# A two-layer graph network on one Trainium2 core: V's weight blocks fetched at other points of the queue, and the first iterations re-ordered

## The chip, the core and the metric

The kernel runs on one core of a Trainium2 chip. A core has TensorE (PE, matrix products; a weight load, PEld, goes with each), VectorE (DVE), ScalarE (ACT), GpSimd (POOL) and SyncE (SP), which here only issues transfers. The metric is the device time of one execution in microseconds (us): 2586.28 us, the median of three runs (2578.19 to 2588.11). The profiled execution has a span of 2589.9 us.

## The reference

Two layers on x (128 batches of 128 tokens and 512 features, float32), each with the batch's own 128x128 mask adj.

```python
# layer 0: attention with 8 heads of 64, then Wo and ReLU
q = (x @ Wq + bq); k = (x @ Wk + bk); v = (x @ Wv + bv)       # split into 8 heads
logits = einsum('bqhd,bkhd->bhqk', q, k) / sqrt(64)
attn = softmax(where(adj > 0, logits, -1e9), axis=-1)
o = einsum('bhqk,bkhd->bqhd', attn, v).reshape(b, n, 512)
x = layernorm(x + relu(o @ Wo + bo))
# layer 1: graph attention with one head
Wh = x @ W
e = leaky(Wh @ a[:512] [:, :, None] + Wh @ a[512:] [:, None, :])   # leaky: slope 0.2
attention = softmax(where(adj > 0, e, -9e15), axis=1)
x = layernorm(x + leaky(attention @ Wh))
```

## The kernel before

Iteration t of the main loop works at once on several batches: the logits and softmax of batch t, attention times V of batch t-1, the product with Wo of the pair that begins at t-3 (odd t), the product with W of the pair that begins at t-6 (even t), the second layer's softmax of batch t-7 and its end. Beside these it makes Q, K and V for the next group of four batches. All instructions of an engine run in the order in which the program writes them.

Every large product is a Strassen product: 7 block products instead of 8. A group's chain works in three PSUM banks, y, w and x, whose roles rotate from chain to chain:

```python
def strassen(bank, multiply, read, add):
    p, t = {}, {}
    def p1():
        p["y"] = bank("y"); multiply(p["y"], 0, True); t[0] = read("t0", p["y"], 0)
    def p5():
        p["w"] = bank("w"); multiply(p["w"], 4, True)
    def p6():
        multiply(p["y"], 5, False); t[2] = read("t2", p["y"], 1)
    def p2():
        p["x"] = bank("x"); multiply(p["x"], 1, True); add(0, 0, p["x"], t[0])
    def p7():
        multiply(p["y"], 6, False); t[3] = read("t3", p["y"], 1); add(1, 1, p["w"], t[3])
    def p4():
        multiply(p["y"], 3, False); add(1, 0, p["y"], None)
    def p3():
        multiply(p["w"], 2, False); add(0, 1, p["w"], t[2])
    return [p1, p5, p6, p2, p7, p4, p3]
```

For a group, one such product is 8 matmuls of 128x128 by 128x256 in the trace. `read` is a ScalarE copy of a bank, `add` a VectorE addition (a ScalarE copy for p4). Wq and Wk with their sums stay on chip; Wv's seven blocks lie in device memory (`wv`) and are fetched for each group into three buffers (`wv_n`):

```python
ring, todo = {}, [0, 4, 5, 1, 6, 3, 2]

def fetch():
    if todo:
        n = todo.pop(0)
        ring[n] = work.tile([P, 2, HALF], F32, name="wv_n", bufs=3)
        nc.sync.dma_start(ring[n], wv[n])

def fetched(n):                 # the weight of V's product n
    fetch()
    return ring.pop(n)

chains = [
    group_product(g, 3 * g, lambda n: wq[:, PLACE[n]], features_first(Q), True, b_cols[:, 0, :]),
    group_product(g, 3 * g + 1, lambda n: wk[:, PLACE[n]], features_first(K), True),
    group_product(g, 3 * g + 2, fetched, tokens_first(V), False),
]
# K's first step also fetches two blocks (cut: with_fetch)
order = [chains[0][n] for n in ((0, 3, 1, 2, 4) if g == 0 else range(5))]
for n in range(2):
    order += [chains[n + 1][0], chains[n][6], chains[n][5]]
    order += chains[n + 1][1:5]
return order + chains[2][5:]
```

The 21 steps of a group are spread over four iterations by `group()`, five in each of three and the rest in the fourth (t a multiple of 4). `pair()` does the same for the seven steps of the products with Wo or W, and `group()` also does up to two "chores": the sums of the weight blocks of Wk, Wv, Wo and W on VectorE, the writes of `wv`, the parts of bo in bf16, the products of W with a.

```python
for t in range(-3, B + 9):
    ...                                       # cut: new steps, load of the mask
    last, sm = sm, Softmax(t) if on(t) else none      # logits of batch t
    while later:
        later.pop(0)()                        # store and 8 spread loads (xz) of the pair's x1
    sm.maxima()
    group()
    ...                                       # cut: second layer
    pair()
    sm.exp(0, 1, 2, 3)
    edge.exp()
    pair()
    sm.exp(4, 5)
    last.transpose()                          # paT of batch t-1
    group()
    sm.reciprocals(0)
    sm.exp(6)
    fin.store()                               # store of the output
    pair()
    sm.exp(7)
    ...
    sm.divide(0, 1, 2, 3)
    group()
    sm.divide(4, 5)
    pair()
    sm.divide(6, 7)
    ...
    copy_o = attend(last) if last is not none else none.copy    # p_oT
    if t % 2 == 0:
        copy_o()
    group()
    sm.spread()                               # pa to device memory and back, as paz
    ...                                       # cut: transposes and loads of x for later groups
    pair(2)
    ...
    group(21 if t % GROUP == 0 else 1)
    fin = Finish(edge) if edge is not none else none
```

x is wanted with features on the partitions. It is loaded in pieces of 512 bytes ("spread", one piece for each block of 32 tokens and quarter of the features) and turned by VectorE in blocks of 32x32. The first four batches, ahead of the loop:

```python
xz = load_pair(0, "pa")                       # batches 0 and 1, spread, SyncE queue
load_blocks(Wq, columns(wq), nc.scalar)
...                                           # b_rows: bq and bv, ScalarE queue
xz2 = load_pair(1, "paz")
load_blocks(Wk, columns(wk), nc.sync)
scale(0); transpose_pair(0, xz)
scale(1); transpose_pair(1, xz2)
sum_x(0)                                      # left sums of x on GpSimd
...                                           # cut: scales and sums of Wq on VectorE
turn_biases()                                 # b_cols: transpose of b_rows on TensorE, two VectorE copies
```

Of the kernel before, what the change touches and what calls it, by code (L numbers as in the profile page):

```python
# [15 lines left out]

H = 8
GROUP = 4
CHORES = 2
EPS = 1e-5  # L20
ALPHA = 0.2
BIG = -1e30
# [3 lines left out]
def kernel(  # L26
# [88 lines left out]
        nc.vector.tensor_scalar_mul(b_cols[:, 0, :], p_b[:, :NC], QSCALE)  # L115
        nc.vector.tensor_copy(b_cols[:, 1, :], p_b[:, NC : 2 * NC])

    def load_blocks(w, columns, queue, spread_rows=True):

        for o, t in enumerate(columns):  # L120
            if spread_rows:
                rows = w.rearrange("(q k c i) (o f) -> o q i k c f", q=4, k=2, c=2, o=2)
                for q in range(4):
                    queue.dma_start(t[32 * q : 32 * q + 32, :, :, :HALF], rows[o, q])
            else:
                rows = w.rearrange("(k c p) (o f) -> o k p c f", k=2, c=2, o=2)
                for k in range(2):
                    queue.dma_start(t[:, k, :, :HALF], rows[o, k])
# [4 lines left out]
    def right_blocks(t):  # L133

        return [
            lambda: nc.vector.tensor_sub(t[2], t[2], t[0]),
            lambda: nc.vector.tensor_sub(t[5], t[3], t[2]),
            lambda: nc.vector.tensor_sub(t[4], t[5], t[0]),
            lambda: nc.vector.tensor_sub(t[6], t[1], t[5]),
        ]  # L140

    def places(w):
        return [w[:, n] for n in range(7)]

    def columns(w):
        return w[:, 0:2], w[:, 2:4]
# [43 lines left out]
    def load_w1():  # L190

        load_blocks(W1, columns(w1), nc.sync)
        a_b = work.tile([P, 2, D], F32, name="a_b", tag="x1T")
        nc.sync.dma_start(
            a_b.rearrange("p s f -> p (s f)"),
            a1.rearrange("f o -> (f o)").partition_broadcast(P),
        )
        sums = small.tile([P, 2, 2, 2, 2], F32, name="wa", bufs=1)

        def dots(k, o, c):  # L200
            def run():
                for s in range(2):
                    scr = work.tile([P, HALF], F32, name="wa_scr", tag="y")
                    nc.vector.scalar_tensor_tensor(
                        scr,
                        w1[:, 2 * o + k, c, :HALF],
                        1.0,
                        a_b[:, s, o * HALF : (o + 1) * HALF],
                        op0=ALU.mult,
                        op1=ALU.mult,  # L210
                        accum_out=sums[:, s, k, o, c : c + 1],
                    )

            return run

        def last_column(k, o):
            def run():
                for c in range(2):
                    nc.vector.tensor_add(
                        w1[:, 2 * o + k, c, HALF:],  # L220
                        sums[:, o, k, 0, c : c + 1],
                        sums[:, o, k, 1, c : c + 1],
                    )

            return run

        every = [(k, o) for k in range(2) for o in range(2)]
        ops = [dots(k, o, c) for k, o in every for c in range(2)]
        return ops + [last_column(k, o) for k, o in every] + right_blocks(places(w1))
# [33 lines left out]
    def sum_x(g):  # L263
        sums = big.tile([P, 3, 2, 2 * P], F32, name="xS")
        XS[g] = left_blocks(XT[g], sums)

    def load_pair(pair, tag):

        z = work.tile([P, 2, 4, P], F32, name="xz2", tag=tag)
        block = x[2 * pair : 2 * pair + 2].rearrange("b (a i) (q e) -> q i (b a) e", i=32, q=4)  # L270
        for q in range(4):
            nc.sync.dma_start(
                z[32 * q : 32 * q + 32].rearrange("p b a e -> p (b a) e"), block[q]
            )
        return z

    def left_blocks(xT, sums):

# [97 lines left out]
    def products(g):  # L376

        for h in range(2):
            Q[g, h] = big.tile([P, NC, HALF], F32, name="qT", bufs=4)
            K[g, h] = big.tile([P, NC, HALF], F32, name="kT", bufs=3)  # L380
            V[g, h] = big.tile([P, 2, D], F32, name="v", bufs=3)

        def features_first(dst):
            return lambda h, o: dst[g, h][:, 2 * o : 2 * o + 2, :]

        def tokens_first(dst):
            return lambda h, o: dst[g, h][:, :, o * HALF : (o + 1) * HALF]
# [6 lines that stand above are left out]
                ring[n] = work.tile([P, 2, HALF], F32, name="wv_n", bufs=3)  # L394
                nc.sync.dma_start(ring[n], wv[n])

        def fetched(n):
            fetch()
            return ring.pop(n)

        chains = [
            group_product(g, 3 * g, lambda n: wq[:, PLACE[n]], features_first(Q), True, b_cols[:, 0, :]),
            group_product(g, 3 * g + 1, lambda n: wk[:, PLACE[n]], features_first(K), True),
            group_product(g, 3 * g + 2, fetched, tokens_first(V), False),
        ]
        fetch_first = chains[1][0]

        def with_fetch():
            fetch_first()
            fetch()  # L410
            fetch()

        chains[1][0] = with_fetch

        order = [chains[0][n] for n in ((0, 3, 1, 2, 4) if g == 0 else range(5))]
        for n in range(2):
            order += [chains[n + 1][0], chains[n][6], chains[n][5]]
            order += chains[n + 1][1:5]
        return order + chains[2][5:]

    def pair_product(xs, w, add, bias=None):
# [294 lines left out]
    group_steps = []  # L716
    later = []
    chores = []
    sm = fin = none

    x_turns = [(), (7, 8), (8,), (8,)]


    xz = load_pair(0, "pa")
    load_blocks(Wq, columns(wq), nc.scalar)
    nc.scalar.dma_start(b_rows[:NC, :], bq.rearrange("(c p) -> c p", p=P))
    nc.scalar.dma_start(b_rows[NC:, :], bv.rearrange("(c p) -> c p", p=P))
    xz2 = load_pair(1, "paz")
    load_blocks(Wk, columns(wk), nc.sync)
    XT[0] = big.tile([P, NC, GROUP * P], F32, name="xT")  # L730

    def transpose_pair(pair, z):
        nc.vector.transpose(
            XT[0][:, :, 2 * pair * P : 2 * (pair + 1) * P].rearrange(
                "p c (b i) -> p b c i", i=32
            ),
            z.rearrange("p b a (c i) -> p (b a) c i", i=32),
        )

    def scale(n):  # L740
        nc.vector.tensor_scalar_mul(wq[:, n], wq[:, n], QSCALE)

    wq_sums = right_blocks(places(wq))
    scale(0)
    transpose_pair(0, xz)
    scale(1)
    transpose_pair(1, xz2)
    sum_x(0)
    scale(2)
    wq_sums[0]()  # L750
    scale(3)
    for op in wq_sums[1:]:
        op()
    turn_biases()
    load_x(4)
    load_x(5)
    chores += right_blocks(places(wk)) + load_wv()
    for t in range(-3, B + 9):
        pair_steps = []
# [7 lines left out]
        def group(n=1):  # L767
            for _ in range(min(n, len(group_steps))):
                group_steps.pop(0)()
            for _ in range(min(CHORES, len(chores))):  # L770
                chores.pop(0)()

        def pair(n=1):
# [2 lines left out]

        if on(t + 1):
            load_mask(t + 1)
        if t == -2:
            load_blocks(Wo, columns(wo), nc.sync, spread_rows=False)  # L780
            more_chores = right_blocks(places(wo)) + load_bias()
        if t == -1:
            chores += more_chores
            more_chores = load_w1()
        if t == 0:
            chores += more_chores

        last, sm = sm, Softmax(t) if on(t) else none
        while later:
            later.pop(0)()  # L790
        sm.maxima()
        group()
        edge = EdgeSoftmax(t - 7) if on(t - 7) else none
        fin.residual()
        if on(t - 2):
            load_residual(t - 2)
        edge.maxima()
        fin.stats()
        if t % GROUP == 0 and on(t + GROUP):
            sum_x(t // GROUP + 1)  # L800
        pair()
        sm.exp(0, 1, 2, 3)
        edge.exp()
        pair()
        sm.exp(4, 5)
        last.transpose()
        group()
        sm.reciprocals(0)
        sm.exp(6)
        fin.store()  # L810
        pair()
        sm.exp(7)
        edge.divide()
        pair()
        sm.reciprocals(1)
        sm.divide(0, 1, 2, 3)
        group()
        sm.divide(4, 5)
        pair()
        sm.divide(6, 7)  # L820
        if on(t + 1):
            mask_float(t + 1)
        copy_o = attend(last) if last is not none else none.copy
        if t % 2 == 0:
            copy_o()
        group()
        sm.spread()
        for b in x_turns[t % GROUP]:
            if on(t + b):
                transpose_x(t + b)  # L830
        for b in x_turns[(t + 1) % GROUP]:
            if on(t + 1 + b):
                load_x(t + 1 + b)
        if on(t + 1):
            mask(t + 1)
        pair(2)
        if t % 2 == 1:
            copy_o()
        if t % 2 == 0:
            for b in (t - 4, t - 3):  # L840
# [44 lines left out]
```

## Time and profile before

| engine or stretch | busy or length |
|---|---|
| TensorE products | 2457.6 us of 2589.9 |
| TensorE products from 134.4 to 2454.3 us | 2266.05 us of 2319.90, granted clock 0.99 |
| before the first product | 13.7 us |
| iteration 0 (48.9 to 69.3 us) | TensorE 15.27, VectorE 16.10, ScalarE 7.95 us of 20.40 |
| iterations 1, 2, 3 | 11.20, 14.20, 17.40 us long |
| iteration 4 (112.1 to 134.4 us) | TensorE 15.11 us of 22.30 |
| after the last group's V (2454.3 us to the end) | TensorE 90.90 us of 135.60 |
| DMA engines from 0 to 20 us | 98% busy, 194 GB/s |

How such lines are read: a row of waits names the engine, tile and line that waited, what released it, the total in us, how often and the longest. A row of a timeline gives start and length, then engine, line, operation, what it writes and reads, and in brackets the idle time just before it and what ended it. SPq is the issue of transfers on SyncE, which takes its entries strictly in order.

### The profile page before, as it was taken

How to read it: one execution, taken by the hardware profiler on the slowest of the kernel's cores; microseconds unless marked ns; L12 is line 12 of the kernel's file. 1: busy time of each engine (PE TensorE's matmuls, PEld its weight loads, DVE VectorE, ACT ScalarE, POOL GpSimd, SP SyncE). 2: the span in 40 equal slices, each digit the busy share in tenths (PEclk: the TensorE clock that was granted, in tenths of full speed). 3: DMA queues.
4: the chain of work that ended last, by engine and by line, in shares of the span. 5: the costliest groups of instructions: out<-in, count | busy, mean ns of one | idle time of the engine just before them, and what ended most of it. 6: DMA issues, size and time to landing. Idle time of an engine off the chain costs nothing.

```text
span 2589.9 us, 43731 instructions
## 1 busy us (share of the span) xinstructions
PE 2457.6 (95%) x13697; PEld 2007.5 (78%) x13697; DVE 1815.5 (70%) x3754; ACT 1440.9 (56%) x5185; POOL 777.7 (30%) x1161
## 2 busy tenths in 40 slices
PE   6899999999999999999999999999999999999975
PEld 5687888888878888888788778888777888887853
DVE  6566777777777776776776667777677777776675
ACT  2555556556556556556565556556555656555651
POOL 1123233323323323323323333323233323233222
PEclk9999999999999999999999999999999999999987
DMA  7444444544544444444544444444444444544431
GB/s 189 142 133 144 162 146 150 162 139 145 165 136 152 162 138 149 161 143 149 165 143 143 146 136 155 164 138 149 153 136 157 158 139 146 162 144 141 150 126 48
DMA packets 352710, 379.90 MB, mean 147 GB/s; under 512 B 39000, under 2 KB 257120, under 8 KB 352480
## 3 DMA queue, kind: packets, MB, share of 16 engines
q1 hardware_dynamic: 351312, 376.07, 45.1%
q8 instruction: 109, 1.79, 0.3%
q10 hardware_dynamic: 1168, 1.05, 0.2%
q14 instruction: 121, 0.99, 0.1%
HBM read 240.91 MB, written 136.05 MB: 146 GB/s over the span
## 4 chain that ended last, share of the span: by engine, by line
PE 67%; DVE 12%; DMA 8%; issue 4%; SPq 3%; ACT 3%; POOL 1%; DVEq 0%; POOLq 0%; ACTq 0%
PE st_y L354 18%; PE p_y L433 12%; PE st_w L354 10%; PE st_x L354 7%; PE p_w L433 6%; PE p_oT L540 4%; PE lg L477 4%; DMA wv_n<-wv 3%; SPq L239 3%; PE p_h L680 3%; DMA x_dram<-x 3%; DVE st L567 3%; PE p_x L433 2%; DVE x L586 2%; DVE xT L244 2%
## 5 line engine op out<-in xcount | busy, mean ns | idle before, releaser
L572 POOL TENSOR_SCALAR ve<-mv 128x1 f32<-128x1 f32 x256 | 68.8, 269 | 1385.4 <-DVE mv L569 1385.4
L498 ACT ACTIVATE pa<-pa,nmax 128x128 f32<-128x128 f32 x1024 | 399.6, 392 | 44.8 <-DVE nmax L492 38.4
L512 ACT ACTIVATE pa<-pa,rs 128x128 f32<-128x128 f32 x1024 | 339.4, 394 | 42.8 <-DVE rs L508 42.8
L553 ACT ACTIVATE oT<-p_oT,b_cols 128x128 f32<-128x128 f32 x512 | 146.0, 368 | 208.5 <-PE p_w L433 203.6
L486 DVE TENSOR_TENSOR pa<-lg,mf 128x512 f32<-128x512 f32 x256 | 164.5, 684 | 102.4 <-PE lg L477 98.2
L331 ACT COPY st_t<-st_y 128x512 f32<-128x512 f32 x192 | 110.5, 575 | 175.6 <-PE st_y L354 171.7
L477 PEld LDWEIGHTS lg<-kT,qT 64*128 64x128 f32 x2048 | 124.2, 187 | 93.7 <-issue 93.7
L498 ACT ACTIVATION_READ_ACCUMULATOR pa<-pa,nmax 128x1 f32 x1024 | 193.3, 189 | 0.0
L444 ACT COPY pr_t<-p_y 128x256 f32<-128x256 f32 (+1 forms) x384 | 140.1, 365 | 88.9 <-PE p_y L433 82.2
L574 POOL TENSOR_TENSOR rstd<-ve,mhalf 128x1 f32<-128x1 f32 x256 | 176.8, 691 | 21.3
L527 DVE STREAM_TRANSPOSE paT<-paz 128x1024 f32<-128x1024 f32 x128 | 159.4, 1245 | 3.3 <-DMA paz<-pa_dram 3.3
L492 DVE TENSOR_REDUCE nmax<-pa 128x8 f32<-128x1024 f32 x128 | 156.2, 1220 | 4.4
L680 PE MATMUL p_h<-wh,att 128*128 128x512 f32 x256 | 133.9, 605 | 17.5 <-DVE att L671 17.5
L640 DVE TENSOR_TENSOR wh<-p_w,pr_t 128x257 f32<-128x257 f32 x128 | 54.6, 426 | 136.3 <-ACT pr_t L444 69.7
L477 PE MATMUL lg<-kT,qT 64*128 64x128 f32 x2048 | 148.7, 285 | 0.0
L335 ACT ACTIVATE st_t<-st_y,b_cols 128x256 f32<-128x256 f32 x192 | 80.6, 471 | 120.8 <-PE st_y L354 120.7
L540 PEld LDWEIGHTS p_oT<-paT,v 128*64 128x64 f32 x2048 | 111.5, 139 | 45.3 <-issue 42.4
L372 DVE TENSOR_TENSOR v<-st_w,st_t 128x512 f32<-128x512 f32 x64 | 44.3, 692 | 144.1 <-ACT st_t L331 85.3
L433 PE MATMUL p_y<-w,x1S 128*128 128x257 f32 x512 | 134.4, 385 | 10.5 <-ACT pr_t L444 10.5
L540 PE MATMUL p_oT<-paT,v 128*64 128x128 f32 x2048 | 142.8, 282 | 1.5 <-DVE paT L527 1.5
L433 PE MATMUL p_y<-wo,oS 128*128 128x256 f32 x512 | 132.6, 382 | 7.1 <-ACT pr_t L444 7.1
L654 ACT ACTIVATE e<-p_e,wh 128x128 f32<-128x128 f32 x128 | 47.3, 370 | 161.3 <-PE p_e L652 161.3
(147 smaller groups left out, 6058.7 us busy)
## 6 DMA issues: line engine op xcount, KB each, us to landing
pa_dram<-pa SPq DMA_DIRECT2D x128, 512.0 KB, 2.6
paz<-pa_dram SPq DMA_DIRECT2D x512, 128.0 KB, 2.7
wv_n<-wv SPq DMA_DIRECT2D x224, 256.0 KB, 2.9
x<-in_x_dram SPq DMA_DIRECT2D x128, 256.0 KB, 3.0
x_dram<-x SPq DMA_DIRECT2D x128, 256.0 KB, 2.0
xz<-x_dram SPq DMA_DIRECT2D x512, 64.0 KB, 2.0
out_dram<-z SPq DMA_DIRECT2D x128, 256.0 KB, 2.1
xz<-in_x_dram SPq DMA_DIRECT2D x496, 64.0 KB, 2.2
```

The costliest lines, as they stand in the source:

```text
L354: nc.tensor.matmul(p[:, m, :], lhs, rhs, start=start and m == 0 and kc == 0, stop=True, skip_group_check=True,)
L433: nc.tensor.matmul(p[:, :width], xs[n][:, kc, :], w[:, PLACE[n], kc, :], start=start and kc == 0, stop=True, skip_group_check=True,)
L477: nc.tensor.matmul(self.lg[r][:, c, :], q[rows, c, cols], k[rows, c, cols], start=True, stop=True)
L486: nc.vector.tensor_add(by_head[:, r * NC : (r + 1) * NC], self.lg[r].rearrange("p c (b k) -> p c b k", b=4), mf.unsqueeze(1).to_broadcast( ...
L492: nc.vector.tensor_reduce(self.nmax, by_head, AX.XY, ALU.max, negate=True)
L498: nc.scalar.activation(self.pa[:, :, h, :], self.pa[:, :, h, :], AF.Exp, bias=self.nmax[:, h : h + 1], accum_out=self.sums[:, h : h + 1],)
L512: nc.scalar.activation(self.pa[:, :, h, :], self.pa[:, :, h, :], AF.Copy, scale=self.rs[:, h : h + 1])
L527: nc.vector.transpose(self.paT.rearrange("p h (a i) -> p a h i", i=32), self.paz.rearrange("p a (h k) -> p a h k", k=32),)
L540: nc.tensor.matmul(p[r * HD : (r + 1) * HD, c, :], v[:, h * HD : (h + 1) * HD], sm.paT[:, r * NC + c, :], start=True, stop=True,)
L553: nc.scalar.activation(OT[pair][:, c, h * P : (h + 1) * P], p[:, c, :], AF.Identity, bias=b_cols[:, 1, c : c + 1],)
L574: nc.gpsimd.tensor_tensor(rstd, ve, mhalf, ALU.pow)
L680: nc.tensor.matmul(p.rearrange("p (o f) -> p o f", o=2), edge.att, wh, start=True, stop=True)
```

## The change

Three things. Within a group, V's blocks are fetched at the end of named steps instead of at the start of V's own, so that block 1 is fetched with K's fourth product (the last step of the third iteration) and not with V's second (in the fourth); and Q's products 4 and 3 change places. The first four batches of x are loaded in whole rows, their features put in order by a VectorE copy, and turned by TensorE with an identity; half of Wq is loaded from the SyncE queue. The iterations before t = 3, which have no product with Wo or W, get a timetable of their own, and the chores are spread otherwise: Wo's from iteration 0, W's from iteration 2. The aim is that TensorE should not wait for V's blocks, for K's bank or for the first data.

```diff
-        def fetched(n):
-            fetch()
-            return ring.pop(n)
...
-            group_product(g, 3 * g + 2, fetched, tokens_first(V), False),
+            group_product(g, 3 * g + 2, ring.pop, tokens_first(V), False),
...
+        def with_fetch(step, n=1):
+            def run():
+                step()
+                for _ in range(n):
+                    fetch()
+            return run
+        chains[1][0] = with_fetch(chains[1][0], 2)
+        chains[2][0] = with_fetch(chains[2][0])
+        chains[1][5] = with_fetch(chains[1][5])
+        for n in (1, 2, 3):
+            chains[2][n] = with_fetch(chains[2][n])
 
         order = [chains[0][n] for n in ((0, 3, 1, 2, 4) if g == 0 else range(5))]
-        for n in range(2):
-            order += [chains[n + 1][0], chains[n][6], chains[n][5]]
-            order += chains[n + 1][1:5]
+        order += [chains[1][0], *chains[0][5:], *chains[1][1:5]]
+        order += [chains[2][0], chains[1][6], chains[1][5], *chains[2][1:5]]
         return order + chains[2][5:]
...
-    xz = load_pair(0, "pa")
-    load_blocks(Wq, columns(wq), nc.scalar)
+    x_rows = [work.tile([P, 2, D], F32, name="x_rows", tag=tag) for tag in ("pa", "paz")]
+    for b in range(GROUP):
+        nc.sync.dma_start(x_rows[b // 2][:, b % 2, :], x[b])
+    load_blocks(Wq, columns(wq), nc.scalar, only=0)
...
-    xz2 = load_pair(1, "paz")
+    load_blocks(Wq, columns(wq), nc.sync, only=1)
...
+    def order_features(b):
+        rows = x_rows[b // 2][:, b % 2, :]
+        turned = work.tile([P, D], F32, name="x_turned", tag="xz", bufs=3)
+        nc.vector.tensor_copy(
+            turned.rearrange("p (c q i) -> p c q i", q=4, c=4),
+            rows.rearrange("p (q c i) -> p c q i", q=4, c=4),
+        )
+        return turned
+    def transpose_rows(b, turned, copy):
+        p = psum("p_x").rearrange("p (c k) -> p c k", c=NC)
+        for c in range(NC):
+            nc.tensor.transpose(p[:, c, :], turned[:, c * P : (c + 1) * P], ident)
+        copy(XT[0][:, :, b * P : (b + 1) * P], p)
...
+    turned = [order_features(b) for b in range(2)]
+    transpose_rows(0, turned[0], nc.vector.tensor_copy)
+    transpose_rows(1, turned[1], nc.scalar.copy)
+    turned.append(order_features(2))
     scale(0)
-    transpose_pair(0, xz)
+    transpose_rows(2, turned[2], nc.scalar.copy)
+    turned.append(order_features(3))
     scale(1)
-    transpose_pair(1, xz2)
+    transpose_rows(3, turned[3], nc.vector.tensor_copy)
+    turn_biases()
     sum_x(0)
...
-            for _ in range(min(CHORES, len(chores))):
+            for _ in range(min(3 * n if t == -3 else n, len(chores))):
                 chores.pop(0)()
...
-        if t == -2:
+        if t == -1:
             load_blocks(Wo, columns(wo), nc.sync, spread_rows=False)
-            more_chores = right_blocks(places(wo)) + load_bias()
-        if t == -1:
-            chores += more_chores
-            more_chores = load_w1()
-        if t == 0:
-            chores += more_chores
+            late_chores = right_blocks(places(wo)) + load_bias()
+        if t == 1:
+            late_chores = load_w1()
+        if t in (0, 2):
+            chores += late_chores
...
+        if t < 3:
+            sm.maxima()
+            group(2)
+            ...
+            sm.exp(0, 1, 2, 3)
+            last.transpose()
+            group()
+            sm.reciprocals(0)
+            sm.exp(4, 5, 6, 7)
+            sm.reciprocals(1)
+            sm.divide(0, 1, 2)
+            group()
+            copy_o = attend(last) if last is not none else none.copy
+            sm.divide(3, 4)
+            copy_o()
+            sm.divide(5, 6, 7)
+            ...
+        else:
+            ...                      # the timetable of before, unchanged
```

More of the change, by code (lines that the diff above doesn't have):

```diff
@@ L18 @@
 GROUP = 4
-CHORES = 2
 EPS = 1e-5
@@ L116, in turn_biases, with load_blocks @@
         nc.vector.tensor_copy(b_cols[:, 1, :], p_b[:, NC : 2 * NC])
-    def load_blocks(w, columns, queue, spread_rows=True):
+    def load_blocks(w, columns, queue, spread_rows=True, only=None):
         for o, t in enumerate(columns):
+            if only not in (None, o):
+                continue
             if spread_rows:
@@ L202, in run @@
                 for s in range(2):
-                    scr = work.tile([P, HALF], F32, name="wa_scr", tag="y")
+                    scr = work.tile([P, HALF], F32, name="wa_scr", tag="x1S")
                     nc.vector.scalar_tensor_tensor(
@@ L265, in sum_x @@
         XS[g] = left_blocks(XT[g], sums)
[L267 to L275, printed above, removed]
     def left_blocks(xT, sums):
@@ L403, in products @@
             group_product(g, 3 * g + 1, lambda n: wk[:, PLACE[n]], features_first(K), True),
-            group_product(g, 3 * g + 2, fetched, tokens_first(V), False),
+            group_product(g, 3 * g + 2, ring.pop, tokens_first(V), False),
         ]
[L406 to L413, printed above, removed]
+        def with_fetch(step, n=1):
[9 more added lines that the diff above has]
+            chains[2][n] = with_fetch(chains[2][n])
         order = [chains[0][n] for n in ((0, 3, 1, 2, 4) if g == 0 else range(5))]
-        for n in range(2):
-            order += [chains[n + 1][0], chains[n][6], chains[n][5]]
-            order += chains[n + 1][1:5]
+        order += [chains[1][0], *chains[0][5:], *chains[1][1:5]]
+        order += [chains[2][0], chains[1][6], chains[1][5], *chains[2][1:5]]
         return order + chains[2][5:]
@@ L718, with x_turns @@
     chores = []
-    sm = fin = none
-    x_turns = [(), (7, 8), (8,), (8,)]
-    xz = load_pair(0, "pa")
-    load_blocks(Wq, columns(wq), nc.scalar)
+    sm = fin = edge = none
+    def x_turns(t):
+        if t < -1:
+            return () if t == -3 else (4, 5, 6)
+        return [b for b in [(), (t + 7, t + 8), (t + 8,), (t + 8,)][t % GROUP] if on(b)]
+    x_rows = [work.tile([P, 2, D], F32, name="x_rows", tag=tag) for tag in ("pa", "paz")]
+    for b in range(GROUP):
+        nc.sync.dma_start(x_rows[b // 2][:, b % 2, :], x[b])
+    load_blocks(Wq, columns(wq), nc.scalar, only=0)
     nc.scalar.dma_start(b_rows[:NC, :], bq.rearrange("(c p) -> c p", p=P))
     nc.scalar.dma_start(b_rows[NC:, :], bv.rearrange("(c p) -> c p", p=P))
-    xz2 = load_pair(1, "paz")
+    load_blocks(Wq, columns(wq), nc.sync, only=1)
     load_blocks(Wk, columns(wk), nc.sync)
     XT[0] = big.tile([P, NC, GROUP * P], F32, name="xT")
[L732 to L737, printed above, removed]
-        )
+    def order_features(b):
[4 more added lines that the diff above has]
+            rows.rearrange("p (q c i) -> p c q i", q=4, c=4),
+        )
+        return turned
[4 more added lines that the diff above has]
+        copy(XT[0][:, :, b * P : (b + 1) * P], p)
     def scale(n):
@@ L753 @@
         op()
-    turn_biases()
-    load_x(4)
-    load_x(5)
     chores += right_blocks(places(wk)) + load_wv()
@@ L790 @@
             later.pop(0)()
[L791 to L824, printed above, removed]
-            copy_o()
-        group()
-        sm.spread()
-        for b in x_turns[t % GROUP]:
-            if on(t + b):
-                transpose_x(t + b)
@@ L831 @@
-        for b in x_turns[(t + 1) % GROUP]:
-            if on(t + 1 + b):
-                load_x(t + 1 + b)
+        if t < 3:
+            sm.maxima()
+            group(2)
+            if on(t - 2):
+                load_residual(t - 2)
+            if t == 0 and on(GROUP):
+                sum_x(1)
+            sm.exp(0, 1, 2, 3)
[8 more added lines that the diff above has]
+            sm.divide(3, 4)
+            copy_o()
+            sm.divide(5, 6, 7)
+            if on(t + 1):
+                mask_float(t + 1)
+        else:
+            sm.maxima()
+            group()
+            edge = EdgeSoftmax(t - 7) if on(t - 7) else none
+            fin.residual()
+            if on(t - 2):
+                load_residual(t - 2)
+            edge.maxima()
+            fin.stats()
+            if t % GROUP == 0 and on(t + GROUP):
+                sum_x(t // GROUP + 1)
+            pair()
+            sm.exp(0, 1, 2, 3)
+            edge.exp()
+            pair()
+            sm.exp(4, 5)
+            last.transpose()
+            group()
+            sm.reciprocals(0)
+            sm.exp(6)
+            fin.store()
+            pair()
+            sm.exp(7)
+            edge.divide()
+            pair()
+            sm.reciprocals(1)
+            sm.divide(0, 1, 2, 3)
+            group()
+            sm.divide(4, 5)
+            pair()
+            sm.divide(6, 7)
+            if on(t + 1):
+                mask_float(t + 1)
+            copy_o = attend(last) if last is not none else none.copy
+            if t % 2 == 0:
+                copy_o()
+            group()
@@ L834 @@
+        sm.spread()
+        for b in x_turns(t):
+            transpose_x(b)
+        for b in x_turns(t + 1):
+            load_x(b)
         if on(t + 1):
@@ L836 @@
         pair(2)
-        if t % 2 == 1:
+        if t % 2 == 1 and t >= 3:
             copy_o()
```

## The prediction

> **What bounds the kernel now.** I read the page's busy line first, then the table of waits of TensorE alone, then the timelines of TensorE and of the SyncE queue around one typical wait, and last the first 135 us in order of time.
>
> ```profile
> PE 2457.6 (95%) x13697; PEld 2007.5 (78%) x13697; DVE 1815.5 (70%) x3754; ACT 1440.9 (56%) x5185; POOL 777.7 (30%) x1161
> ...
> PE st_x L354 <- DMA wv_n<-wv: 55.3, 31, 6.5
> PE p_y L433 <- ACT pr_t L444: 19.2, 9, 5.0
> PE p_h L680 <- DVE att L671: 17.5, 3, 6.6
> PE p_b L114 <- DMA b_rows<-in_L_gnn_bv_dram: 13.7, 1, 13.7
> PE st_w L354 <- ACT qT L335: 7.6, 30, 1.6
> PE st_y L354 <- ACT st_t L331: 5.8, 3, 2.6
> PE st_y L354 <- issue: 3.8, 2, 2.8
> ```
>
> TensorE is busy 95% of the span and no other engine over 70%, so a microsecond in which TensorE stands still is a microsecond of the span. The waits (total, times, longest) say where it stands. The first row is the great one: `st_x<-wv_n`, the fourth product of V's chain, waits for the fetch of Wv's block 1 in 31 of the 32 groups. The `qT` row is small but comes in 30 groups. `p_y` and `p_h` lie mostly after 2470 us, where no group is left; the change does not touch them. The others lie before 135 us.
>
> Why that fetch is late shows in a steady group (TensorE, then the SyncE queue; columns are start and length in us):
>
> ```profile
> 1278.01 1.03 PE L433 MATMUL p_y<-w,x1S 128*128 128x257 f32 x4
> 1278.88 1.03 PE L433 MATMUL p_x<-w,x1T 128*128 128x257 f32 x4
> 1282.26 1.99 PE L354 MATMUL st_x<-wv_n,xT 128*128 128x256 f32 x8 [2.35 <-DMA wv_n<-wv]
> ```
>
> ```profile
> 1272.34 0.34 SPq L594 DMA_DIRECT2D x_dram<-x  x1
> 1272.72 0.43 SPq L456 DMA_DIRECT2D adj<-in_adj_dram  x1
> 1273.65 1.03 SPq L594 DMA_DIRECT2D x_dram<-x  x1
> 1275.79 3.64 SPq L239 DMA_DIRECT2D xz<-x_dram  x8
> 1279.53 0.38 SPq L395 DMA_DIRECT2D wv_n<-wv  x1
> ```
>
> The block's buffer has long been free (V's first product ended some 16 us before), yet its fetch is issued at 1279.53, behind a store that waits for a normalisation and behind eight issues of 3.64 us that wait for that store to land. The fetch then takes 2.7 us. So this is a place in a queue, not a lack of buffers or of bandwidth.
>
> **What the Trainium skill says.** "Perfetto Trace Analysis", Identifying Performance Opportunities: a gap that repeats on the engine that should be saturated can mean too few buffers. Here the gap repeats, but the trace names another cause, the queue's order. The same page, Identifying the Most-Contended Engine, warns that matmul busy share says little of the distance to the limit; I therefore go by waits and not by the 95%. "TensorE: Matmul & The Clock Gate", Part 1: the array's clock is halved after an idle window of about 3.4 us and needs about as long to return. The trace agrees in kind: of the 31 waits, seven (6.51, 2.92, 3.01, 3.39, 1.91, 3.19 and 3.75 us) are followed by a `st_x` of 3.4 to 3.8 us in place of 1.99, though 1.91 us was once enough and 3.44 us once was not. So a wait can cost more than itself. "DMA: Bandwidth & Descriptors", Issuing engines are not separate DMA queues: issuing from ScalarE and SyncE saves only issue time. So shifting half of Wq from one queue to the other can change which data come first, not how fast they come; in the first 20 us the DMA engines are 98% busy in the trace.
>
> **Part 1: the fetches of V.** The number of fetches stays 7 a group. The order of instructions of the changed kernel shows block 1's fetch on the SyncE queue after the first `x_dram` store and ahead of `adj`, the second store and the eight `xz` issues. By the timeline it would be issued at about 1272.7 instead of 1279.5 and land at 1275.4; the product could begin at 1279.9 (1282.26 - 2.35), so it has 4 us to spare. The wait goes: 55.3 us. With it goes the slow clock after seven of them: (3.60+3.44+3.68+3.78+3.50+3.52+3.53) - 7 x 1.99 = 11.1 us. Sum 66.4 us.
> What takes its place: block 6 now stands in the queue where block 1 stood, and lands where block 1 did. Its product comes after `st_x` (1.73 us at the usual spacing), one pair product (0.86) and `p_oT` (1.02), 3.6 us after `st_x` could start. The median wait of block 1 was about 1.2 us, the longest in the steady part 3.75. So block 6 is in time in all but one or two groups. Blocks 3 and 2 come 0.9 and 4 us later and are wanted 3.5 and 7 us later. I give back 5 us for such cases and for waits of ScalarE or VectorE that the gap used to hide. Net 61 us.
>
> **Part 2: Q's last two products change places.** Before, Q's product 4 (the one that frees bank `y`) ran immediately before K's second product, which takes that bank, and ScalarE's read-out had to fit between. Afterwards product 3 stands between, 1.73 us. The 30 waits go: 7.6 us. Product 4 itself needs only ScalarE's copy of `t3`, and K's first product still lies between. Net 7 us.
>
> **Part 3: the start.** The first product of the first group begins at 13.87 us, slow; the first logits come 35 us later, at 48.92, with 30.4 us of products between.
>
> ```profile
> 13.87 3.75 PE L354 MATMUL st_y<-xT,wq 128*128 128x256 f32 x8
> 17.45 1.91 PE L354 MATMUL st_x<-xT,wq 128*128 128x256 f32 x8
> 19.19 1.89 PE L354 MATMUL st_w<-xS,wq 128*128 128x256 f32 x8
> 23.92 3.40 PE L354 MATMUL st_y<-xS,wq 128*128 128x256 f32 x8 [2.84 <-issue]
> ...
> 57.98 3.38 PE L354 MATMUL st_y<-wv_n,xS 128*128 128x256 f32 x8 [2.53 <-ACT st_t L331]
> 63.97 2.56 PE L354 MATMUL st_y<-wv_n,xT 128*128 128x256 f32 x8 [2.60 <-ACT st_t L331]
> ```
>
> Added are 16 TensorE transposes of 128x128 (273 ns alone for the same operation in `p_e`, about 0.11 us apart back to back; estimate 16 x 0.25 = 4 us with the slow clock), four feature-order copies and four evacuations, 128x512, about 0.65 us each, six of the eight on VectorE: 4 us. Removed are two VectorE transposes of 1.24 us. All of this starts when x comes, and x now comes in whole rows, in front of all but half of Wq, 1.5 MB where 2 MB stood before it. At the 194 GB/s of the first 20 us, 1.5 MB is 7.7 us; with the last copy, transposes and evacuation about 10.5 us. So the first product starts 3 us earlier. b_cols is now computed ahead of the Wq sums (before, ScalarE waited for it until 21.7 us, then loaded its table for 1.28 us, and the fourth product could begin only at 23.9), which I count at 4 us; the gaps before the fifth product and K's second, and the rest of the slow clock, 2 us. The first logits then come near 40 us: 9 us.
> Iteration 0 lasts 20.4 us before (48.92 to 69.31) for 1.1 + 6 x 1.73 = 11.5 us of products; the late ones wait for ScalarE's copies behind exponentials that themselves wait for VectorE, which is doing bias parts and the products with a. Fewer extra jobs there and two steps before the exponentials: I expect 15.5 us, so 5 us. Iteration 2's wait of 1.3 us for `p_oT`: 1 us. Against it, the 16 products with a (551 ns each, 8.8 us of VectorE) and the W sums now fall into iterations 2 to 4, where VectorE has its softmax: I charge 2 us. Net 9 + 5 + 1 - 2 = 13 us.
>
> **Sum.** 61 + 7 + 13 = 81 us. 2586.3 - 81 = 2505 us, a gain of 3.1%.
>
> **The rivals.**
> (a) Another wait takes the gap's place: block 6's fetch, or ScalarE's `st_t` for the fifth product, or VectorE's `paT` for `p_oT`. For: everything near this point is tightly packed, and the copy of `st_t` sits among exponentials. Against: in the group shown `st_t` ended at 1280.1 and is wanted at 1283.5, `paT` ended at 1280.4 and is wanted at 1282.5; and the other three iterations of a group run without any wait. If half of the gap came back, 61 becomes 30 and the time 2536.
> (b) The start gets no better: TensorE's transposes run slow, VectorE takes on 4 us where it was already the one waited for, or DMA, at 98%, decides. The write-out of Wv could also come too late for V's first product. For: the share of DMA. Against: fewer bytes precede the first product. Part 3 would be 0 and the time 2518.
> (c) TensorE, denser, is granted less clock. Against: from 134 to 2454 us it is busy 2266 of 2320 us at a clock of 0.99, and the low clocks lie only after gaps. If it lost 2% of those 2320 us, the gain would fall to 35 us: 2551.
> (d) Better than thought: no give-back and a first logit at 36 us: 2494.
>
> **Range and chances.** The 66 us of part 1 rest on a named wait and a place in a queue that the changed order shows gone; part 3 is the soft term, 0 to 20 us. With (a) half true I get 2536, with (d) and a kinder start about 2485. Range 2484 to 2536. A gain of over 2% means below 2534.6: chance 0.88. Within 2%: 0.10. Slower by over 2%: 0.02.
>
> **What would show it.** Right: the row `st_x <- DMA wv_n` is gone from TensorE's waits and no `wv_n` row over 10 us stands there; its `qT` row is gone; `st_x` products of over 3 us are gone in the steady part; a group takes 75.6 us (76.9, the spacing of groups with a wait near 1.07, less 1.07 and 0.2) where the mean was 77.7; the first logits begin at 38 to 42 us and those of iteration 1 at 54 to 58 us. Wrong: a new row `st_y <- DMA wv_n` of tens of us (a), first logits after 46 us (b), a clock below 0.97 in the steady part (c).

## The result, and the profile after

The changed kernel takes 2515.36 us (median of four runs, 2512.16 to 2516.03). The ratio to the kernel before is 0.9723 (95% interval 0.9693 to 0.9753), a gain of about 72 us. Run again with the last experiments it gave 0.9706 (0.9692 to 0.9720). Foreseen were 2505 us and a gain of 81.

TensorE's share of busy time and the chain that ended last, from the page of the changed kernel, then the waits of TensorE alone (total, times, longest, in us):

```profile
PE 2444.2 (97%) x13713; PEld 2000.3 (80%) x13713; DVE 1817.5 (72%) x3758; ACT 1429.8 (57%) x5187; POOL 781.1 (31%) x1161
...
PE 92%; DVE 3%; DMA 2%; ACT 1%; issue 1%; SPq 1%; POOL 0%; DVEq 0%; POOLq 0%; ACTq 0%
```

```profile
PE p_y L425 <- ACT pr_t L436: 20.3, 11, 5.0
PE p_h L672 <- DVE att L663: 17.6, 3, 6.6
PE p_x L743 <- DVE x_turned L733: 8.0, 4, 5.2
PE p_oT L532 <- DVE paT L519: 3.6, 4, 1.8
PE st_y L345 <- ACT pa L504: 2.6, 1, 2.6
PE st_y L345 <- ACT st_t L322: 2.4, 2, 1.7
PE st_y L345 <- DMA wv_n<-wv: 1.8, 2, 1.6
...
PE st_x L345 <- DMA wv_n<-wv: 0.7, 1, 0.7
```

The great row of before, 55.3 us of `st_x` for block 1, is 0.7 us and one occurrence. The `qT` row is gone. The two rows now on top lie in the last iterations, as before (but for one wait of 0.75 us). In the chain TensorE has 92% where it had 67%.

One steady group of the changed kernel, TensorE and the SyncE queue (start, length):

```profile
1317.08 1.03 PE L425 MATMUL p_x<-w,x1T 128*128 128x257 f32 x4
1317.95 1.89 PE L345 MATMUL st_x<-wv_n,xT 128*128 128x256 f32 x8
1319.67 1.03 PE L425 MATMUL p_y<-w,x1S 128*128 128x257 f32 x4
1320.63 1.09 PE L532 MATMUL p_oT<-paT,v 128*64 128x128 f32 x16
```

```profile
1310.53 0.34 SPq L586 DMA_DIRECT2D x_dram<-x  x1
1310.97 0.38 SPq L386 DMA_DIRECT2D wv_n<-wv  x1
1311.40 0.45 SPq L448 DMA_DIRECT2D adj<-in_adj_dram  x1
1311.90 0.43 SPq L586 DMA_DIRECT2D x_dram<-x  x1
1312.62 3.99 SPq L240 DMA_DIRECT2D xz<-x_dram  x8
1316.71 0.38 SPq L386 DMA_DIRECT2D wv_n<-wv  x1
```

Block 1 (first `wv_n`) is issued at 1310.97, 7 us before `st_x` begins, without a gap. Block 6 (second `wv_n`) stands where block 1 stood, and is issued 5 us ahead of its product. From group to group `st_x` is now 75.63 us apart, the same to 0.02 us for 28 groups; before it was 76.8 to 80.5 from the third group on.

The first logits begin at 43.25 us (before 48.92), those of iterations 1 to 5 at 57.31, 69.80, 83.84, 102.24 and 121.64 (before 69.31, 80.45, 94.66, 112.07, 134.28). So 12.6 us of the gain are in by iteration 5, and the fetch has its part in them.

### The profile page after: what moved, and what is told of

Read it like the earlier page. It is cut to its first block, busy times and chain, and to the rows that moved or that the text cites. A ratio compares the mean times of both kernels' runs of the same rounds, so it can differ in the third digit from the quotient of the medians.

```text
span 2513.0 us, 43768 instructions
## 1 busy us (share of the span) xinstructions
PE 2444.2 (97%) x13713; PEld 2000.3 (80%) x13713; DVE 1817.5 (72%) x3758; ACT 1429.8 (57%) x5187; POOL 781.1 (31%) x1161
## 4 chain that ended last, share of the span: by engine, by line
PE 92%; DVE 3%; DMA 2%; ACT 1%; issue 1%; SPq 1%; POOL 0%; DVEq 0%; POOLq 0%; ACTq 0%
PE st_y L345 26%; PE p_y L425 17%; PE st_w L345 13%; PE p_w L425 8%; PE st_x L345 7%; PE lg L469 5%; PE p_oT L532 5%; PE p_h L672 4%; PE p_x L425 4%; ACT pa L490 1%; PE p_e L643 1%; PE p_e L644 1%; DMA wv_n<-wv 0%; ACT pa L504 0%; DVE st L559 0%
## 5 line engine op out<-in xcount | busy, mean ns | idle before, releaser
L469 PEld LDWEIGHTS lg<-kT,qT 64*128 64x128 f32 x2048 | 124.2, 187 | 93.7 <-issue 93.7
L425 PE MATMUL p_y<-w,x1T 128*128 128x257 f32 x512 | 135.4, 387 | 1.0 <-ACT pr_t L436 1.0
```

The source lines that it names most:

```text
L425: nc.tensor.matmul(p[:, :width], xs[n][:, kc, :], w[:, PLACE[n], kc, :], start=start and kc == 0, stop=True, skip_group_check=True,)
L469: nc.tensor.matmul(self.lg[r][:, c, :], q[rows, c, cols], k[rows, c, cols], start=True, stop=True)
```

## The experiments

The theory to be tested: block 1's place in the SyncE queue carries the gain, Q's exchange brings 7 us and the start 13. The rivals: buffers or bandwidth made the fetch late; the start is what let the rest gain; and, as the start gave less than foreseen, either the moved jobs for W or the softmax of iteration 4 is in the way. In the tables, ratios are to the kernel before, run beside it on the same chip.

### Each part alone

**e1_fetch_only.** The new fetch points on the kernel before, Q's order kept:

```diff
-            group_product(g, 3 * g + 2, fetched, tokens_first(V), False),
+            group_product(g, 3 * g + 2, ring.pop, tokens_first(V), False),
+        chains[1][0] = with_fetch(chains[1][0], 2)
+        chains[2][0] = with_fetch(chains[2][0])
+        chains[1][5] = with_fetch(chains[1][5])
+        for n in (1, 2, 3):
+            chains[2][n] = with_fetch(chains[2][n])
```

> The kernel before with only the fetch points of V moved; Q's order, the first loads and the timetable stay. If block 1's place in the queue carries the gain: about 60 us less than before (2525 to 2530), no wv_n row over 10 us, 75.8 us for a group. If the gain needs the dense start: under 30 us. Iteration 4 tells apart why the start gave less than foreseen: about 19 us long here too, if the chain of the softmax sets it once the fetch does not (it was hidden under the fetch); 14 to 15 us, if the jobs for W that the change moves there set it (they are not moved here).

**e2_swap_only.** The kernel before with

```diff
-        for n in range(2):
-            order += [chains[n + 1][0], chains[n][6], chains[n][5]]
-            order += chains[n + 1][1:5]
+        order += [chains[1][0], *chains[0][5:], *chains[1][1:5]]
+        order += [chains[2][0], chains[1][6], chains[1][5], *chains[2][1:5]]
```

> The kernel before with only Q's products 4 and 3 exchanged. If the wait for bank y is a cost of its own: the qT row of TensorE's waits goes, 7 us less than before (2580). If the fetch behind it in the same group takes up whatever is gained (the fetch then is late by that much more): the row goes, the wv_n row grows by about as much in the groups, and the time is the same within 3 us.

**e3_start_only.** The changed kernel with the fetch points and the order of before (the reverse of both edits above).

> The changed kernel with the fetch points and Q's order of before: the start alone. Prediction: 13 us less than before. By the profile of the changed kernel: about 12 us less at the first logits of iteration 1, and what is left at iteration 5 tells the rest: 5 us less than before if later iterations give 7 back; iteration 4 as long as before (22 us).

**e4_act_queue.** The kernel before with

```diff
-                nc.sync.dma_start(ring[n], wv[n])
+                (nc.scalar if n == 1 else nc.sync).dma_start(ring[n], wv[n])
```

> The kernel before with block 1 alone issued from ScalarE instead of SyncE: same program point, same three buffers, same bytes. If only the place behind the stores and the spread loads made it late: the wv_n row falls from 55 to under 10 us, 45 to 60 us less than before (2527 to 2542). If buffers or the DMA engines' bandwidth made it late: the row stays over 40 us and the time within 10 us of before.

| kernel | median us | ratio, 95% interval | `wv_n` rows | a steady group |
|---|---|---|---|---|
| e1_fetch_only | 2521.89 | 0.9762 (0.9736 to 0.9788) | 0.8 | 75.56 |
| e2_swap_only | 2588.53 | 1.0018 (1.0003 to 1.0033) | 50.2 | 76.7 to 79.8 |
| e3_start_only | 2576.34 | 0.9973 (0.9962 to 0.9983) | 51.1 | 76.6 to 79.8 |
| e4_act_queue | 2530.53 | 0.9799 (0.9775 to 0.9824) | 2.9 | mostly 75.56 |

The fetch points alone bring 61 us (0.0238 x 2583), with nothing of the dense start. e4 says why: with the same program point, buffers and bytes, and only another queue for one block, the wait is gone and 52 us with it. So neither buffers nor bandwidth made it late, but what stood ahead of it in SyncE's queue. (The 9 us less than in e1 were not taken apart; block 6, which keeps its place in e4, is waited for in 4 groups, and iteration 4 takes 22.7 us, in e1 19.3.) The Trainium skill ("DMA: Bandwidth & Descriptors", Issuing engines are not separate DMA queues) says that issuing from several engines only saves the time of issuing. Here it also took a transfer out from behind others that were themselves waiting; on this point the measurement decides.

The exchange alone brings nothing; by the times it is 0.2% slower. Its `qT` row is gone, as foreseen, and the `wv_n` row did not grow (50.2 after 55.3; the row scatters, with 50.5 and 56.7 in e5 and e6, which have the fetch and the order of before). So neither reading of the expectation is borne out. The steady groups of e1 and of the changed kernel show where the wait went. In e1, without the exchange, TensorE, then ScalarE:

```profile
1289.84 1.03 PE L435 MATMUL p_y<-w,x1S 128*128 128x257 f32 x4
1290.80 1.09 PE L542 MATMUL p_oT<-paT,v 128*64 128x128 f32 x16
1292.06 1.99 PE L354 MATMUL st_w<-xS,wk 128*128 128x256 f32 x8 [0.17 <-ACT qT L335]
```

```profile
1288.85 0.35 ACT L446 COPY pr_t<-p_y 128x257 f32<-128x257 f32 x1
...
1291.19 0.82 ACT L335 ACTIVATE qT<-st_y,b_cols 128x256 f32<-128x256 f32 x2
```

And in the changed kernel, with it:

```profile
1280.84 1.89 PE L345 MATMUL st_w<-xT,wq 128*128 128x256 f32 x8
1282.80 1.11 PE L425 MATMUL p_y<-w,x1S 128*128 128x257 f32 x4
1283.84 1.09 PE L532 MATMUL p_oT<-paT,v 128*64 128x128 f32 x16
```

```profile
1281.20 0.81 ACT L326 ACTIVATE qT<-st_y,b_cols 128x256 f32<-128x256 f32 x2
1281.91 0.39 ACT L490 ACTIVATE pa<-pa,nmax 128x128 f32<-128x128 f32 x1
...
1282.30 0.36 ACT L436 COPY pr_t<-p_y 128x257 f32<-128x257 f32 x1
```

Q's copy (0.81 us) has moved ahead of the pair product's copy `pr_t`. That copy now ends at 1282.66 and its product `p_y` begins at 1282.80, 0.23 us after the products before it make room (1280.84 + 1.73). By the same count the wait for `qT` in e1 is 0.24 us: 1.26 us lie between the starts of `p_oT` and `st_w`, and 1.02 in the changed kernel, where `st_w` waits for nothing. So a wait of 0.24 us has become one of 0.23 us. Only 0.07 us of it lie behind the end of the products before (1280.84 + 1.89), and the table of waits doesn't name it. In e2, where the fetch is still late, it stands at the same new place, with 1.96 us between the two starts:

```profile
1324.01 1.89 PE L354 MATMUL st_w<-xT,wq 128*128 128x256 f32 x8
1325.97 1.11 PE L432 MATMUL p_y<-w,x1S 128*128 128x257 f32 x4
```

A group takes 75.63 us with the exchange in the changed kernel and 75.56 without it in e1.

### The start, taken apart

**e5_rows_only.** The kernel before with the changed kernel's first loads, transposes and split of Wq (the whole stretch from `x_rows` to the sums of Wq, then `load_x(4)` and `load_x(5)` as before).

> The kernel before with only the first loads of the changed one: whole rows, feature order on VectorE, transposes on TensorE, half of Wq on the other queue; timetable and V's fetches of before. First product near 12.5 us, as in the changed kernel, instead of 13.9; the fourth product near 19.5 instead of 23.9; first logits 4 to 6 us earlier than before. If no later wait takes it up: 4 to 6 us less than before; if block 1's late fetch or VectorE's extra jobs in iteration 0 take it up: same within 2 us.

**e6_timetable_only.** The changed kernel with `load_pair` and `transpose_pair` of before in that stretch, and V's fetches and Q's order of before.

> The kernel before with only the other timetable of iterations -3 to 2 and the moved extra jobs; first loads and V's fetches of before. Iteration 0 falls from 20.4 to 14 or 15 us; iterations 3 and 4 together no shorter than before. If the moved jobs for W cost as much as the timetable gains: same within 3 us; if they cost little: 5 to 7 us less than before.

**e7_w_jobs_early.** The changed kernel with

```diff
-        if t == 1:
-            late_chores = load_w1()
-        if t in (0, 2):
-            chores += late_chores
+        if t == 0:
+            chores += late_chores
+            late_chores = load_w1()
+        if t == 1:
+            chores += late_chores
```

> The changed kernel with W's extra jobs from iteration 1 instead of 2. If these jobs on VectorE are what made iterations 3 and 4 wait: iteration 3 back to 17.4 us, iteration 4 from 19.4 to 15 or 16, in all 4 to 5 us less than the changed kernel (2511). If the chain of the softmax sets iteration 4: 3 and 4 together within 1 us of the changed kernel, and iterations 1 and 2 longer.

**e8_iter4.** The changed kernel with

```diff
-        if t < 3:
+        if t < 3 or t == 4:
...
-            if t == 0 and on(GROUP):
-                sum_x(1)
+            if t % GROUP == 0 and on(t + GROUP):
+                sum_x(t // GROUP + 1)
```

> The changed kernel with iteration 4 (which has no pair product yet) on the timetable of iterations 0 to 2: two of V's products, and ScalarE's copies for them, ahead of the exponentials. If ScalarE's copies behind the exponentials are the wait of iteration 4: from 19.4 to about 17 us, 2 to 3 us less than the changed kernel (2513). If VectorE's moved jobs are: no change.

Lengths of the iterations, from the begin of the logits of one to those of the next, in us:

| kernel | first logits at | 0 | 1 | 2 | 3 | 4 | ratio, 95% interval |
|---|---|---|---|---|---|---|---|
| before | 48.92 | 20.4 | 11.1 | 14.2 | 17.4 | 22.2 | 1 |
| changed | 43.25 | 14.1 | 12.5 | 14.0 | 18.4 | 19.4 | 0.9723 (0.9693 to 0.9753) |
| e1_fetch_only | 47.74 | 21.0 | 11.1 | 13.7 | 17.4 | 19.3 | 0.9762 (0.9736 to 0.9788) |
| e3_start_only | 44.34 | 13.6 | 12.5 | 17.1 | 17.4 | 24.8 | 0.9973 (0.9962 to 0.9983) |
| e5_rows_only | 44.62 | 20.2 | 11.1 | 13.5 | 17.4 | 22.3 | 0.9989 (0.9980 to 0.9999) |
| e6_timetable_only | 49.37 | 13.6 | 12.5 | 15.5 | 17.4 | 22.5 | 1.0011 (0.9998 to 1.0025) |
| e7_w_jobs_early | 43.92 | 22.6 | 15.6 | 11.2 | 18.2 | 23.0 | 0.9767 (0.9744 to 0.9791) |
| e8_iter4 | 44.71 | 13.7 | 12.5 | 14.1 | 18.4 | 21.0 | 0.9739 (0.9718 to 0.9761) |

The rows of x (e5) bring 4.3 us at the first logits, with the first and the fourth product at 12.36 and 19.54 us as foreseen, and about 3 us of the time. The timetable (e6) takes 6.8 us off iteration 0 and gives 1.4 back in iteration 1 and 1.3 in iteration 2. At iteration 5 e6 is 3.4 us ahead, of which the times keep nothing; with the fetch late in every later group I can't say more of so small a difference.

What holds iteration 4? In e1 the moved jobs for W are not there, and in e7 all but two of 0.7 us are over by then; yet it takes 19.3 and 23.0 us (in e7 with two slow products). So it is not they. Nor is it the softmax, as I had thought next. TensorE in the changed kernel:

```profile
107.78 1.99 PE L345 MATMUL st_x<-wv_n,xT 128*128 128x256 f32 x8 [0.73 <-DMA wv_n<-wv]
110.42 1.09 PE L532 MATMUL p_oT<-paT,v 128*64 128x128 f32 x16 [0.65 <-DVE paT L519]
114.07 3.22 PE L345 MATMUL st_y<-wv_n,xS 128*128 128x256 f32 x8 [2.55 <-ACT pa L504]
117.96 2.02 PE L345 MATMUL st_y<-wv_n,xT 128*128 128x256 f32 x8 [0.68 <-ACT st_t L322]
```

and ScalarE and the SyncE queue ahead of 114.07, where V's fifth product begins, the one that needs block 6:

```profile
111.49 0.56 ACT L322 COPY st_t<-st_y 128x512 f32<-128x512 f32 x1
...
112.73 2.43 ACT L504 ACTIVATE pa<-pa,rs 128x128 f32<-128x128 f32 x8
```

```profile
107.07 3.80 SPq L240 DMA_DIRECT2D xz<-x_dram  x8
110.97 0.59 SPq L386 DMA_DIRECT2D wv_n<-wv  x1
```

The product needs ScalarE's copy `st_t`, which ended at 112.05. It does not need `pa`, which the row names as releaser. Block 6 was issued at 110.97, behind the eight spread loads, and the product began 3.1 us later. In the other kernels the same product begins 2.8 us (e1: 119.59 to 122.43) and 3.5 us (e7: 120.62 to 124.08) after that issue; a fetch of this size takes 2.9 us in the median. So it is block 6 that ended the wait, under another name. f1, below, names it openly:

```profile
116.00 1.97 PE L345 MATMUL st_y<-wv_n,xS 128*128 128x256 f32 x8 [3.02 <-DMA wv_n<-wv]
```

There is no product with W yet in iteration 4, so TensorE comes to the fifth product sooner after the logits than in a steady group, and the queue is not faster. In e8, TensorE comes sooner still, and the wait is longer:

```profile
109.17 1.99 PE L345 MATMUL st_x<-wv_n,xT 128*128 128x256 f32 x8 [1.07 <-DMA wv_n<-wv]
115.45 3.75 PE L345 MATMUL st_y<-wv_n,xS 128*128 128x256 f32 x8 [4.28 <-DMA wv_n<-wv]
```

e7 shows the same fault by another way. It issues W's eight loads in iteration 0, where they and the load of a stand between V's fetches:

```profile
41.16 0.91 SPq L386 DMA_DIRECT2D wv_n<-wv  x2
42.11 0.43 SPq L448 DMA_DIRECT2D adj<-in_adj_dram  x1
42.58 7.62 SPq L125 DMA_DIRECT2D w<-in_L_gnn_W_dram  x8
50.25 0.43 SPq L195 DMA_DIRECT2D a_b<-in_L_gnn_a_dram  x1
51.52 1.56 SPq L386 DMA_DIRECT2D wv_n<-wv  x3
```

Iteration 0 takes 22.6 us, with 4.32 us of waiting for block 6 and that product and the next one slow (3.75 and 3.78 us), and the kernel 2526.37 us. For iteration 4 the moved jobs were the wrong suspect; W's loads in iteration 0 cost more than they save.

### The exchange again, the end, and iteration 4

**after_again** is the changed kernel once more.

> The changed kernel once more, for the comparison with the three that follow: 2515 us, 75.63 us for a group.

**f1_no_swap.** The changed kernel with

```diff
-        order += [chains[1][0], *chains[0][5:], *chains[1][1:5]]
-        order += [chains[2][0], chains[1][6], chains[1][5], *chains[2][1:5]]
+        for n in range(2):
+            order += [chains[n + 1][0], chains[n][6], chains[n][5]]
+            order += chains[n + 1][1:5]
```

> The changed kernel with Q's last two products in the order of before. If the exchange only moved the wait (from K's second product to the pair product after it, whose ScalarE copy now stands behind the copy of Q): 75.56 us for a group, 0 to 3 us less than the changed kernel. If the exchange saves its 7 us once the fetch is out of the way: 75.8 us for a group, 7 us more.

**f2_tail.** f1 with, in the timetable from t = 3,

```diff
-            pair()
+            pair(1 if t < B - 3 else 3)
             sm.exp(0, 1, 2, 3)
```

> The kernel without the exchange, and in the last iterations (from t = 125, where no group is made any more) three pair products at once ahead of the exponentials, so that ScalarE's second copy for them (pr_t) precedes the exponentials. If that copy's place is the wait: the pr_t row falls from 20 us to under 8, 8 to 20 us less than without (2495 to 2507). If the chain of softmax and transfers sets the last iterations: the row falls and others rise, within 3 us.

**f3_iter4.** f2 with e8's edit and

```diff
-                nc.sync.dma_start(ring[n], wv[n])
+                queue = nc.scalar if g == 1 and n == 6 else nc.sync
+                queue.dma_start(ring[n], wv[n])
```

> As the run before, and iteration 4 on the timetable of iterations 0 to 2, with block 6 of this one group issued from ScalarE, so that it doesn't wait behind the spread loads. If block 6's place in the queue was what undid that timetable alone: no wv_n wait of over 1 us in iteration 4, which falls from 19.4 us to 16 or 17; 2 to 4 us less than the run before. If another chain sets it: 19 us still.

| kernel | median us | ratio, 95% interval | a group | iterations 0 to 4 |
|---|---|---|---|---|
| after_again | 2517.10 | 0.9706 (0.9692 to 0.9720) | 75.63 | 13.6, 12.5, 14.4, 18.4, 21.1 |
| f1_no_swap | 2516.47 | 0.9702 (0.9685 to 0.9720) | 75.56 | 13.6, 12.5, 15.5, 17.4, 18.3 |
| f2_tail | 2512.39 | 0.9692 (0.9677 to 0.9706) | 75.56 | 13.6, 12.5, 17.1, 17.4, 18.4 |
| f3_iter4 | 2512.35 | 0.9689 (0.9675 to 0.9702) | 75.56 | 13.6, 12.5, 17.2, 17.4, 16.6 |

Without the exchange the time is the same; it moves about a microsecond between iterations 2 and 3, no more. Iteration 4 of the changed kernel takes 21.1 us here and took 19.4 before: the waits are alike (2.56 and 2.55 us ahead of the fifth product), but here the product after it was slow (3.78 us in place of 2.02). A difference of 2 us between two profiles of iteration 4 therefore means something only where no product in it is slow, as in f1, f2 and f3.

In f2 the `pr_t` row falls from 19.5 to 11.8 us, and 5.6 us come up in two other rows, one new and one that was 0.4:

```profile
PE p_h L673 <- DVE att L664: 17.5, 3, 6.6
PE p_y L426 <- ACT pr_t L437: 11.8, 7, 4.0
...
PE p_w L426 <- DVE rt L663: 3.9, 2, 3.0
...
PE p_w L426 <- DVE pr_t L606: 2.1, 1, 2.1
```

From the last group's `st_x` to TensorE's last product it is 124.8 us in f2 and 124.2 in f1, and the medians of the two, 4 us apart, lie within the scatter of f1 (2511.27 to 2519.39). So it is the second reading that fits: the last iterations have another bound than that copy's place; which, these runs don't show. In f3, with e8's timetable and block 6 issued from ScalarE, the fifth product no longer waits and iteration 4 takes 16.6 us, against 18.4 in f2; with that timetable alone (e8) it waited 4.28 us for the block. So block 6's place was the cause there. Blocks 1 and 3, still in SyncE's queue, are waited for 1.92 and 1.47 us, so the expected absence of waits over 1 us was not met. f3 has the lowest ratio of all, but its interval overlaps with the changed kernel's. I do not call it faster.

## Why the prediction was right, and where it was off

**Part 1** (61 us net of 66 gross): right. The row is gone, and alone it brought 61 us (interval 55 to 68). Block 6 was in time in every steady group, so rival (a) failed there; it was late in one place, iteration 4, as the give-back foresaw for "one or two groups". There the late block 1 and the slow clock after it had cost 8.1 us (6.51 + 3.60 - 1.99), and in e1 the iteration became 2.9 us shorter (22.2 to 19.3). The other 5.2 went to block 6 (2.72 us and, by the slow clock after it, 3.56 - 1.99) and to what was left of block 1's wait (0.84).

**Part 2** (7 us): wrong. "Product 3 stands between" was true and the 30 waits went, but the step from 7.6 us of waits to 7 us of time failed. I had looked at TensorE's order alone. (Of the 7.6 us, 2.5 lay in the first iterations, as 0.93 and 1.59 us; in a steady group the row was 0.17 us, so that the other iterations of a group were not wholly without a wait, as rival (a) has it.) The same exchange moved a 0.81 us copy on ScalarE ahead of one that another product waits for. Measured 0: alone 0.2% slower, and within the changed kernel 0.9706 with it, 0.9702 without.

**Part 3** (13 us): the mechanism held, the size was off. Alone (e3) the start brought 7 us (0.0027 x 2583; 4 to 10): it was 11.4 us ahead at the logits of iteration 1 and 4.5 at iteration 5, for iteration 2 was 2.9 us longer than before and iteration 4, with 8.46 us of waiting for the late block 1 in place of 6.51, 2.6. Comparing f1 with e1, which differ by the start alone and both have the fetch on time, iteration 5 begins 8.0 us earlier (122.29 against 130.32; two profiles of the changed kernel differ there by 1.65 us). Term by term, in the changed kernel:

- the first product, foreseen at 10.5 us: 12.55. The fourth feature-order copy stands behind a scaling of Wq in VectorE's order, and that waited for Wq until 10.49 us; so the last transposes began at 11.30. In VectorE's and SyncE's lines:

```profile
10.49 0.43 DVE L747 TENSOR_SCALAR wq<-wq 128x512 f32<-128x512 f32 x1 [2.49 <-DMA wq<-in_L_gnn_Wq_dram]
10.83 0.42 DVE L733 COPY x_turned<-x_rows 128x512 f32<-128x512 f32 x1
```

```profile
2.58 6.38 SPq L125 DMA_DIRECT2D wq<-in_L_gnn_Wq_dram  x4
```

By 10.49 us the DMA engines had moved about 2.1 MB (an estimate: 204 GB/s in the trace over 10.49 us), not the 1.5 MB of the prediction. The half of Wq in SyncE's queue was issued from 2.58 us on, so it could take its share beside the half that was counted as ahead of it. This is read from the trace and not tested.

- the first logits, foreseen at 40 us: 43.25. Besides those 2 us, V's first product waited 1.6 us for its block, which rival (b) had named.
- iteration 0, foreseen 15.5 us: 14.1, better.
- the rest (1 us off, 2 us on): 1.4 us on in iteration 1, 0.2 off in iteration 2, 1.0 on in iteration 3. The wait of iteration 2 for `p_oT`, which was to go, is 1.82 us. `paT` stands on VectorE directly behind four of the products with a, which take it from 77.85 to 79.68:

```profile
80.89 1.09 PE L532 MATMUL p_oT<-paT,v 128*64 128x128 f32 x16 [1.82 <-DVE paT L519]
```

```profile
79.60 1.24 DVE L519 STREAM_TRANSPOSE paT<-paz 128x1024 f32<-128x1024 f32 x1
```

The 1.0 us of iteration 3 is not due to the jobs for W alone: with them and without the exchange it takes 17.4 us in f1. But iteration 2 then takes 15.5, so no run separates what these jobs cost in iterations 2 and 3 together.

**Sum.** 61 + 0 + 8 = 69 us, against 72 measured and 81 foreseen. Rival (c), less clock for a denser TensorE, did not come: 0.989 over the span, 0.983 before, and 1.00 between 140 and 2400 us. A group came out at 75.63 us, foreseen 75.6.

## What to carry to other kernels

When a repeated gap ends on a transfer, read the issuing queue just before it: if the buffer was free and other transfers that were themselves waiting stood ahead, move the issue to an earlier point or another queue before buying buffers. A wait that leaves the table is saved time only if no other wait lay under it and if the edit moved nothing on the engines that feed its neighbours, so check the order of all engines, not only of the one that waited. And where the releaser that a row names is nothing the instruction needs, look up when each of its real inputs was ready; here it was a transfer.

## What the runs showed that was not expected

After TensorE's 16 transposes from 5.18 us on, the first product was still slow: its eight matmuls, at 12.55, took 3.51 us where 1.89 to 1.99 is usual. The Trainium skill, "TensorE: Matmul & The Clock Gate", Part 4, says that transposes don't count as busy in the same way. No run here shows that this was the reason: the transposes were spread over 7 us with gaps, and the granted clock reads 1.00 from 12.5 to 16.1 us, where it reads 0.60 beside the slow product at 114.07. And a pipeline with no wait in it is very even: 28 groups in a row within 0.02 us of each other, where with the fetch late they scattered over 3.7 us.
